# Norm statistics on VectorE or ScalarE, and new ranks for the strands of a two-layer kernel

## The chip, the cores and the metric

The kernel runs on one core of one Trainium2 chip. The metric is the device time of one execution in microseconds, as the median of several runs. A profile of one execution comes with it.

## The reference

Two transformer layers run one after the other over 16 sequences of 256 tokens with 128 features, 4096 tokens in all, in float32. Each half of a layer is followed by a residual sum and a layer norm:

```python
x = _layernorm(x + _L0_attn_ref(x, ...))   # RMS norm, 16 heads of 64, softmax over 256 keys, output projection
x = _layernorm(x + _L0_ffn_ref(x, ...))    # router, top 2 of 8 experts (hidden 256), one shared expert, exact gelu
x = _layernorm(x + _L1_attn_ref(x, ...))   # 16 heads of 8; each token attends over its own 16 heads
x = _layernorm(x + _L1_ffn_ref(x, ...))    # router, top 2 of 8 experts (hidden 512), exact gelu

def _layernorm(x, axis=-1, eps=1e-05):
    m = jnp.mean(x, axis=axis, keepdims=True)
    v = jnp.var(x, axis=axis, keepdims=True)
    return (x - m) / jnp.sqrt(v + eps)
```

The norm has neither scale nor shift, and its mean and variance go over the 128 features of a token.

## The kernel before

The tokens are cut into eight groups of 512. A group lies in SBUF as a tile `xg[g]` of 128 partitions by 4 chunks by 128 features, so that one chunk is 128 tokens, one on each partition. Layer 0's attention (`attention0`) goes through the groups in order, in 128 units: a unit is two heads of one sequence, with its scores, softmax, transposes and weighted values. `project` makes the output projection and `summed` adds the residual and calls the norm. The last group is cut in two halves (`project2`, `summed2`).

While attention still runs, finished groups go on to the experts of layer 0 in five waves (`wave`): the router chooses two experts for each token (`route`), `send` scatters the tokens' rows by indirect DMA from POOL into lists that are sorted by expert, `lists` runs the experts' matmuls over the lists, and `gathered` fetches the two results of each token and adds them. `middle` then calls the norm, layer 1's attention (`attention1`, with `chunk1` for each chunk, mostly products and sums on VectorE and POOL) and the second norm, and layer 1's experts follow in three waves (`wave1`, `last`), with the third norm and the store of the output. The second half of the last group goes through all experts without lists (`sequence`, `dense`).

All these are strands: Python generators that issue instructions for one step and then yield the time and the engine of their next one. `everything` is the planner. It keeps a clock for each engine (`clk`), booked by `work(engine, us, ...)` with a cost written into the code, and always continues the strand whose next step could start first; a strand's key is a rank and a time offset. The offset is taken off a strand's start when strands are compared, and ranks decide ties:

```python
best = min(starts, key=lambda c: (max(c[0] - c[1].key[0], first), c[1].key[1:]))[1]
```

The constants `KEYS` hold (rank, offset) for each kind of strand, `PACE` the offset of layer 0's heads in each half group. The order that comes out is the program order of every engine's queue, fixed when the kernel is built. Where a step may run on either of two engines, the planner's clocks decide: `copied` compares VectorE and ScalarE with `COPY` added to VectorE's side, `chunk1` gives products to POOL or VectorE by `FAVOUR` and lets TensorE make sums when it is `SUMS` behind VectorE, and `SWITCH` and `SWITCH_BACK` delay steps that need another activation table.

`normed(y, o, tag, at)` is called 36 times, nine in each of four places, for 32 chunks in each (128 in all; a call has four chunks or two). It takes its statistics on VectorE at L391 and L393, then `powered` adds eps at L377 on VectorE and raises to the power -0.5 at L381 on POOL, and the result is applied on VectorE (L399) or, after two small POOL operations (L405, L406), on ScalarE (L409). The RMS norm of layer 0 (`normalised`) sums its squares on ScalarE at L474, with the accumulator output. Softmax takes its maxima at L537 on VectorE and exponentials at L543 on ScalarE. The attention of layer 1 has products at L1216 and L1292 and sums at L1220 and L1267. L270 and L272 are the two roads of `copied`, L905 the scatter, L934 the gather, L948 the sum after a gather. PSUM has two buffers for each of its three tags "s", "t" and "m".

Of the kernel before, what the change touches and what calls it, by code (L numbers as in the profile page):

```python
# [9 lines left out]
FP = mybir.dt.float32  # L10
AF = mybir.ActivationFunctionType
ALU = mybir.AluOpType
# [3 lines left out]
P = 128  # L16
D = 128
# [20 lines left out]
def two_layers(  # L38
# [23 lines left out]
    nc = tc.nc  # L62
# [7 lines left out]
    sm = ctx.enter_context(tc.tile_pool(name="sm", bufs=2))  # L70
# [67 lines left out]
    def cleared(layer, w):  # L138
# [10 lines left out]

    INF = float("inf")  # L150
    KEYS = {
        "copy qk": (-0.897, 0.036),
        "copy v": (-2, 0.466),
        "copy p": (0.219, 0.818),
        "copy o": (-2, 0.246),
        "softmax": (-0.178, 0.347),
        "softmax 2": (-1.887, 0.235),
        "summed": (-1.203, 0.424),
        "normalised": (-0.822, 0.486),
        "heads": (-0.667, 0.044),  # L160
        "w route": (0.515, 0.015),
        "w send": (0.14, 0.346),
        "w shared": (-0.361, 0.219),
        "w loads": (-0.176, 0.409),
        "w turns 0": (-1.078, 0.086),
        "w turns 1": (1.714, 0.284),
        "w firsts 0": (-1.18, 0.141),
        "w firsts 1": (-0.671, 0.597),
        "w gelu": (-0.639, 0.186),
        "w seconds 0": (-0.71, 0.566),  # L170
        "w seconds 1": (-0.947, -0.095),
        "w stored": (-0.148, -0.464),
        "w gathered 0": (0.897, 0.302),
        "w gathered 1": (1.266, -0.485),
        "w qkv": (2, 0.577),
        "w attention1": (0.922, 0.081),
        "w attention1 2": (0.862, 0.231),
        "w sums": (0.434, 0.099),
        "w normed": (-1.109, 0.178),
        "d loads": (0.367, 1.088),  # L180
        "d route": (-0.611, 0.589),
        "d firsts": (-0.264, -0.008),
        "d gelu": (0.669, 0.244),
        "d seconds": (0.433, -0.444),
        "d added": (0.222, 0.651),
        "d normed": (-0.464, 0.567),
    }
    PACE = [0.305, 1.929, -0.337, -0.416, 1.268, -0.017, 0.106, 1.867]
    PACE += [1.673, 1.567, 1.23, 2, 1.49, 1.385, 1.46, 2]
    now = [0]  # L190
    COPY = -0.089
    SUMS = 9.857
    FAVOUR = 0.474
    SWITCH, SWITCH_BACK = 0.249, 0.734
    window, unit = [0, 0.0, 1.0], [P]
    clk = {"PE": 0.0, "DVE": 0.0, "ACT": 0.0, "POOL": 0.0, "SP": 0.0}
    table = ["exp"]
# [10 lines left out]
    def paced(at, us, mode):  # L208

        if mode != unit[0]:  # L210
            unit[0] = mode
            us += 0.09
        w = int(at / W)
        if w > window[0]:
            window[2] = 2.0 if w > window[0] + 1 or window[1] < 0.6 * W else 1.0
            window[:2] = w, 0.0
        us *= window[2]
        while at + us > (w + 1) * W:
            part = (w + 1) * W - at
            window[1] += part  # L220
            left = (us - part) / window[2]
            window[2] = 2.0 if window[1] < 0.6 * W else 1.0
            w, at, us = w + 1, (w + 1) * W, left * window[2]
            window[:2] = w, 0.0
        window[1] += us
        return at + us

    def work(e, us, *after, ports=False, one=None, mode=P):

        at = max(clk[e], floor[0], *after)  # L230
        if ports and pool[0] - 0.15 > at:
            us += min(pool[0] - 0.15 - at, pool[1])
        clk[e] = (paced(at, us, mode) if e == "PE" else at + us) + SETUP[e]
        if one is not None:
            pool[:] = clk[e], one
        return clk[e] + 0.08
# [23 lines left out]
    EITHER = ("DVE", "ACT")  # L260

    def copied(o, i, *after):
# [5 lines left out]
        dve, act = (max(clk[e], *after) + t for e, t in zip(EITHER, us))  # L268
        if dve + COPY <= act:
            nc.vector.tensor_copy(o, i)  # L270
# [102 lines left out]
    def powered(var, scale, eps, tag, at):  # L373

        n = var.shape[1]
        v = sm.tile([P, n], FP, tag=f"{tag}_v", name=f"{tag}_v", bufs=1 if tag == "ln0" else 2)
        nc.vector.tensor_scalar(v, var, scale, eps, ALU.mult, ALU.add)  # L377
        at = work("DVE", 0.2, at)
        yield at, "POOL"
        r = sm.tile([P, n], FP, tag=f"{tag}_r", name=f"{tag}_r", bufs=1 if tag == "ln0" else 2)  # L380
        nc.gpsimd.tensor_tensor(r, v, mhalf[:, 0:n], ALU.pow)  # L381
        return r, work("POOL", 1.1, at)

    def normed(y, o, tag, at):

        n = y.shape[1]
        yield at, "DVE"
        st = sm.tile([P, n, 6], FP, tag=f"{tag}_st", name=f"{tag}_st", bufs=1 if tag == "ln0" else 2)
        mv = sm.tile([P, n, 2], FP, tag=f"{tag}_mv", name=f"{tag}_mv", bufs=1 if tag == "ln0" else 2)
        for c in range(n):  # L390
            nc.vector.bn_stats(st[:, c, :], y[:, c, :])  # L391
        for c in range(n):
            nc.vector.bn_aggr(mv[:, c, :], st[:, c, :])  # L393
        at = work("DVE", 0.43 * n, at)
        r, at = yield from powered(mv[:, :, 1], 1.0, 1e-5, tag, at)
        yield at, EITHER
        if max(clk["DVE"], at) + 1.9 <= max(clk["ACT"], at) + 1.4:
            for c in range(n):
                nc.vector.tensor_scalar(  # L399
                    o[:, c, :], y[:, c, :], mv[:, c, 0:1], r[:, c : c + 1], ALU.subtract, ALU.mult  # L400
                )
            return work("DVE", 0.05 + 0.35 * n, at, ports=True)

        nb = sm.tile([P, n], FP, tag=f"{tag}_nb", name=f"{tag}_nb", bufs=1 if tag == "ln0" else 2)
        nc.gpsimd.tensor_tensor(nb, mv[:, :, 0], r, ALU.mult)  # L405
        nc.gpsimd.tensor_scalar(nb, nb, -1.0, 1.0, ALU.mult, ALU.mult)  # L406
        at = work("POOL", 0.4, at)
        for c in range(n):
            nc.scalar.activation(o[:, c, :], y[:, c, :], AF.Identity, bias=nb[:, c : c + 1], scale=r[:, c : c + 1])  # L409
        return work("ACT", 0.35 * n, at)  # L410
# [56 lines left out]
    def normalised(g):  # L467
# [10 lines left out]
        yield at, EITHER  # L478
        if max(clk["DVE"], at) + 1.2 + COPY <= max(clk["ACT"], at) + 1.4:
            for c in range(NC):  # L480
# [16 lines left out]
        hT[g] = sb.tile([P, GT], FP, tag="hT", name=f"hT{g}")  # L497
        if max(clk["DVE"], at) + 0.75 + COPY <= max(clk["ACT"], at) + 0.7:
            nc.vector.tensor_scalar(hT[g], t, nscale_s, None, ALU.mult)
# [136 lines left out]
    def summed(g, half, place, py, at):  # L636
        yield at, "DVE"
        nc.vector.tensor_tensor(ya[g], py, ya[g] if half else xg[g], ALU.add)
        at = closed(place, work("DVE", 0.75, at))
        if half:  # L640
            end["x", g] = yield from normed(ya[g], xg[g], "ln0", at)
# [16 lines left out]
    def summed2(b, place, py, at):  # L658
        yield at, "DVE"
        x = xg[LAST][:, 2 * b : 2 * b + 2, :]  # L660
        y = sb.tile([P, 2, D], FP, tag="ya", name=f"ya{LAST}_{b}", bufs=1)
        nc.vector.tensor_tensor(y, py, x, ALU.add)
        at = closed(place, work("DVE", 0.45, at))
        end["x", LAST, b] = yield from normed(y, x, "ln0", at)

    def attention0():
# [3 lines left out]
        for u in range(len(UNITS) + LAG):  # L670
# [4 lines left out]
            if g < NG:  # L675
                now[0] = 2 * g + i // NP
                running[-1].key = (KEYS["heads"][1], PACE[now[0]], 0, 0)
                if i == 3 and g + 1 < NG:
# [522 lines left out]
    def chunk1(w, c, o, qv, kv, at, sums):  # L1201
# [5 lines left out]
        for j in range(2):  # L1207
            yield (lambda: max(at, prod_ring.free(), sc_ring.free() if j == 0 else 0.0)), "DVE"
            if j == 0:
                sc1, ks = sc_ring.tile([P, NH1, NH1], "sc")  # L1210
                if "over" in end and clk["PE"] + SUMS < max(clk["DVE"], at) and ends["s"][-2] < clk["PE"] + 1.0:
                    ps = ps_s.tile([P, NH1, NH1], FP, tag="s", name="s1")
# [29 lines left out]
        if place is None:  # L1242
            yield at, ("POOL", "DVE")
            e, us = ("POOL", 0.6) if max(clk["POOL"], at) <= max(clk["DVE"], at) + FAVOUR else ("DVE", 0.4)
            (nc.gpsimd if e == "POOL" else nc.vector).tensor_tensor(
# [39 lines left out]
        for j in range(2):  # L1285
            yield (lambda: max(at, prod_ring.free())), ("POOL", "DVE")
            e, us = "POOL", 2.35
            if max(clk["DVE"], at) + 1.25 + FAVOUR < max(clk["POOL"], at) + 2.35:
                e, us = "DVE", 1.25
# [8 lines left out]
            at2 = work("POOL", us, at, one=us) if e == "POOL" else work("DVE", us, at, ports=True)  # L1298
            if j == 0 and "over" in end and clk["PE"] + SUMS < max(clk["DVE"], at) and ends["s"][-2] < clk["PE"] + 1.0:
                po = ps_s.tile([P, P], FP, tag="s", name="o1_sums")  # L1300
# [177 lines left out]
    w = DENSE  # L1478
# [185 lines left out]
```

## Time and profile before

| | before |
|---|---|
| median of 4 runs | 1225.72 us (1223.81 to 1227.38) |
| profiled execution | 1224.7 us |
| its span, first to last instruction | 1223.0 us |
| mean granted TensorE clock | 0.962 |
| busy: TensorE, VectorE, ScalarE, POOL | 1095.6, 911.1, 730.7, 701.8 us |
| norm statistics L391 | 64 + 32 + 32 instructions, 276 ns median |
| norm aggregates L393 | 96 + 32 instructions, about 150 ns median |
| activation table loads | 64, 1283 ns each |

The page of a profile gives busy time of each engine and its share of the span, then the span in 40 equal slices, where each digit is a busy share in tenths. Lines of a group name the kernel's line, the engine, the operation, its output and inputs and the count; behind the bar stand busy time, mean duration and the idle time before the group with what ended it. Matmul records are pipelined, so a busy TensorE need not be at its peak. Durations of neighbouring instructions of one engine can overlap, so a sequence is measured from its first start to its last end.

### The profile page before, as it was taken

How to read it: one execution, taken by the hardware profiler on the slowest of the kernel's cores; microseconds unless marked ns; L12 is line 12 of the kernel's file. 1: busy time of each engine (PE TensorE's matmuls, PEld its weight loads, DVE VectorE, ACT ScalarE, POOL GpSimd, SP SyncE). 2: the span in 40 equal slices, each digit the busy share in tenths (PEclk: the TensorE clock that was granted, in tenths of full speed). 3: DMA queues.
4: the chain of work that ended last, by engine and by line, in shares of the span. 5: the costliest groups of instructions: out<-in, count | busy, mean ns of one | idle time of the engine just before them, and what ended most of it. 6: DMA issues, size and time to landing. Idle time of an engine off the chain costs nothing.

```text
span 1223.0 us, 22539 instructions
## 1 busy us (share of the span) xinstructions
PE 1095.6 (90%) x7272; PEld 793.7 (65%) x7272; DVE 911.1 (75%) x1810; ACT 730.7 (60%) x2073; POOL 701.8 (57%) x1085
## 2 busy tenths in 40 slices
PE   9999999989999999988999998898667889778893
PEld 5566667666656665576655666675466879678792
DVE  4767786449889888864788888978886979896333
ACT  6556566667657756666566666765554655454441
POOL 4434363635565547732864775577684745476765
PEclk9999999999999999999999999999787989899997
DMA  8900021441000003043000033315627977975871
GB/s 266 274 1 1 1 83 57 143 117 56 6 1 1 2 1 93 29 127 92 30 1 2 16 106 104 94 46 168 189 87 235 282 213 216 273 218 170 248 227 58
DMA packets 187207, 132.45 MB, mean 108 GB/s; under 512 B 12745, under 2 KB 171474, under 8 KB 187090
## 3 DMA queue, kind: packets, MB, share of 16 engines
q1 hardware_dynamic: 179410, 115.27, 31.9%
q0 software_dynamic: 7680, 15.74, 4.1%
q8 instruction: 58, 0.95, 0.3%
q14 instruction: 59, 0.48, 0.1%
HBM read 97.94 MB, written 33.03 MB: 107 GB/s over the span
## 4 chain that ended last, share of the span: by engine, by line
PE 61%; DVE 13%; POOL 11%; ACT 7%; issue 4%; DMA 3%; SPq 1%; ACTq 0%; POOLq 0%; DVEq 0%
PE s L574 10%; PE po L612 9%; PE t L591 8%; POOL rows L905 7%; PE po_e L1118 4%; PE ph L1098 4%; PE pv L528 4%; PE pq L510 4%; PE py L629 3%; PE pk L510 3%; POOL pr L558 2%; DVE qk_prod L1216 2%; DVE av_prod L1292 2%; PE po_d L1541 1%; ACT h L1077 1%
## 5 line engine op out<-in xcount | busy, mean ns | idle before, releaser
L558 POOL TENSOR_SCALAR pr<-pr,rs 128x256 f32<-128x256 f32 x512 | 247.2, 502 | 258.2 <-DVE rs L554 169.6
L543 ACT ACTIVATE pr<-s,nm 128x256 f32<-128x256 f32 x512 | 236.1, 476 | 12.2 <-DVE nm L537 10.5
L537 DVE TENSOR_REDUCE nm<-s 128x4 f32<-128x1024 f32 x128 | 156.2, 1220 | 59.5 <-PE s L574 59.0
L1098 PE MATMUL ph<-xqT,wa 128*128 128x128 f32 x1028 | 142.5, 295 | 22.7 <-ACT h L1077 9.0
L905 POOL DMA_INDIRECT rows<-x,r_pi x120 | 132.1, 1101 | 39.5 <-issue 20.8
L1098 PEld LDWEIGHTS ph<-xqT,wa 128*128 128x128 f32 x1028 | 133.3, 206 | 32.2 <-ACT h L1077 11.6
L934 POOL DMA_INDIRECT y<-outs,r_pi x120 | 122.1, 1017 | 52.5 <-issue 22.6
L591 PE MATMUL t<-ident,pr 128*128 128x128 f32 x1024 | 141.8, 279 | 5.2 <-ACT pT L272 1.9
L591 PEld LDWEIGHTS t<-ident,pr 128*128 128x128 f32 x1024 | 111.4, 141 | 48.6 <-POOL pr L558 23.0
L612 PE MATMUL po<-pT,v 128*64 128x256 f32 x1024 | 140.5, 393 | 2.2 <-DVE kT L270 0.9
L270 DVE COPY pT<-t 128x512 f32<-128x512 f32 x171 | 111.6, 685 | 34.5 <-PE t L591 34.1
L574 PEld LDWEIGHTS s<-kT,qT 64*128 64x128 f32 x896 | 77.1, 186 | 82.3 <-issue 65.8
L574 PE MATMUL s<-kT,qT 64*128 64x256 f32 x896 | 127.1, 402 | 0.0
L272 ACT COPY oT<-po 128x256 f32<-128x256 f32 x102 | 38.0, 373 | 135.7 <-PE po L612 135.5
L543 ACT ACTIVATION_READ_ACCUMULATOR pr<-s,nm 128x1 f32 x512 | 106.0, 207 | 0.0
L1292 POOL TENSOR_TENSOR av_prod<-sc,qkv 128x1024 f32<-128x1024 f32 x34 | 86.2, 2545 | 29.3 <-ACT sc L1254 28.9
L612 PEld LDWEIGHTS po<-pT,v 128*64 128x64 f32 x1024 | 62.9, 136 | 61.8 <-issue 17.6
L1216 DVE TENSOR_TENSOR qk_prod<-qkv 128x1024 f32<-128x1024 f32 x64 | 83.0, 1297 | 0.0
L1267 DVE TENSOR_REDUCE o<-av_prod 128x64 f32<-128x1024 f32 x64 | 75.8, 1200 | 8.5 <-POOL av_prod L1292 8.2
L1118 PE MATMUL po_e<-wb,h 128*128 128x128 f32 x648 | 78.0, 279 | 2.0 <-DVE lg L738 1.5
L1220 DVE TENSOR_REDUCE sc<-qk_prod 128x128 f32<-128x1024 f32 x64 | 78.1, 1220 | 2.2
L1118 PEld LDWEIGHTS po_e<-wb,h 128*128 128x128 f32 x648 | 76.0, 195 | 3.6 <-DVE lg L738 1.9
(230 smaller groups left out, 1968.2 us busy)
## 6 DMA issues: line engine op xcount, KB each, us to landing
wa<-in_w_dram SPq DMA_DIRECT2D x190, 128.0 KB, 2.2
wa<-in_w_dram SPq DMA_DIRECT2D x81, 256.0 KB, 3.3
wb<-in_w_dram SPq DMA_DIRECT2D x81, 256.0 KB, 4.1
xq<-rows SPq DMA_DIRECT2D x38, 256.0 KB, 3.4
outs<-yq SPq DMA_DIRECT2D x38, 256.0 KB, 3.6
rows<-clear SPq DMA_DIRECT2D x3, 1472.0 KB, 11.6
rows<-clear SPq DMA_DIRECT2D x1, 2496.0 KB
rows<-clear SPq DMA_DIRECT2D x2, 1216.0 KB
```

The lines of the kernel that those rows point to most:

```text
L270: nc.vector.tensor_copy(o, i)
L537: nc.vector.tensor_reduce(nm[u], s, AX.X, ALU.max, negate=True)
L543: nc.scalar.activation(pr[u][:, i, :], s[:, i, :], AF.Exp, bias=nm[u][:, i : i + 1], accum_out=su[u][:, i : i + 1],)
L558: nc.gpsimd.tensor_scalar(pr[u][:, i, :], pr[u][:, i, :], rs[:, i : i + 1], 1.0, ALU.mult, ALU.mult)
L574: nc.tensor.matmul(sc[u][:, j, qc, :], q[part, ts(qc, P)], k[part, :], start=True, stop=True,)
L591: nc.tensor.transpose(t[:, kc, ts(qc, P)], pr[u][:, 2 * j + qc, ts(kc, P)], ident)
L612: nc.tensor.matmul(po[j * DH : (j + 1) * DH, :], vs[g, p // 4, 2 * b + kc][:, ts(h, DH)], pT[u][j][:, kc, :], start=(kc == 0), stop=(kc == 1),
L905: i = nc.gpsimd.indirect_dma_start(out=rows[layer][w][:, :], out_offset=bass.IndirectOffsetOnAxis(ap=r.pos[:, k, c : c + 1], axis=0), in_= ...
L934: nc.gpsimd.indirect_dma_start(out=y, out_offset=None, in_=outs[layer][w][:, :], in_offset=bass.IndirectOffsetOnAxis(ap=r.pos[:, k, c0 + c ...
L1098: nc.tensor.matmul(ph[:, q - q0, c, :], was[i, q][0][:, c, :], xTs[i][0][:, q, :], start=True, stop=True)
L1118: nc.tensor.matmul(po[:, q, :], hs[i, q][0][:, c, :], wbs[i, q][0][:, c, :], start=(c == 0), stop=(c == nh - 1))
L1292: (nc.gpsimd if e == "POOL" else nc.vector).tensor_tensor(m, sc1[:, ts(j, HALF)].unsqueeze(2).to_broadcast(full), v3.unsqueeze(1).to_broad ...
```

## The change

`normed` gets a second road for its statistics. If by the planner's clocks ScalarE would be through sooner, it makes two passes over each chunk there: Identity with a scale of -1/128 and the accumulator output, which gives the negative mean, and then Square with that as the bias and the accumulator output, which gives the sum of squares around the mean. `powered` then works on these sums, and the result is applied on VectorE or, after one POOL operation instead of two, on ScalarE. The constants of the planner are new.

```diff
     KEYS = {
-        "softmax": (-0.178, 0.347),
-        "softmax 2": (-1.887, 0.235),
-        "summed": (-1.203, 0.424),
+        "softmax": (0.123, 0.534),
+        "softmax 2": (-2, 0.288),
+        "summed": (-1.973, 0.291),
...
-        "w attention1": (0.922, 0.081),
-        "w attention1 2": (0.862, 0.231),
-        "w sums": (0.434, 0.099),
-        "w normed": (-1.109, 0.178),
+        "w attention1": (0.503, 0.205),
+        "w attention1 2": (0.398, 0.088),
+        "w sums": (-0.064, 0.324),
+        "w normed": (-0.698, 0.178),
...
     }
-    PACE = [0.305, 1.929, -0.337, -0.416, 1.268, -0.017, 0.106, 1.867]
-    PACE += [1.673, 1.567, 1.23, 2, 1.49, 1.385, 1.46, 2]
+    PACE = [1.119, 1.936, -0.517, -0.529, 1.723, 1.03, 0.706, 1.646]
+    PACE += [1.833, 1.427, 0.658, 0.868, 1.747, 1.411, 1.4, 0.455]
     now = [0]
-    COPY = -0.089
-    SUMS = 9.857
-    FAVOUR = 0.474
-    SWITCH, SWITCH_BACK = 0.249, 0.734
+    COPY = 0.465
+    SUMS = 8.497
+    FAVOUR = -0.257
+    SWITCH, SWITCH_BACK = 0.937, 0.586
...
     def normed(y, o, tag, at):
 
         n = y.shape[1]
-        yield at, "DVE"
+        yield at, EITHER
+        if max(clk["ACT"], at) + 1.0 * n < max(clk["DVE"], at) + 0.43 * n:
+
+            mm = sm.tile([P, 2, n], FP, tag=f"{tag}_mm", name=f"{tag}_mm", bufs=1 if tag == "ln0" else 2)
+            junk = sm.tile([P, D], FP, tag="junk", name="junk", bufs=1)
+            for c in range(n):
+                nc.scalar.activation(junk, y[:, c, :], AF.Identity, scale=-1.0 / D, accum_out=mm[:, 0, c : c + 1])
+            for c in range(n):
+                nc.scalar.activation(
+                    junk, y[:, c, :], AF.Square, bias=mm[:, 0, c : c + 1], accum_out=mm[:, 1, c : c + 1]
+                )
+            at = work("ACT", 1.0 * n, at)
+            yield at, "DVE"
+            r, at = yield from powered(mm[:, 1, :], 1.0 / D, 1e-5, tag, at)
+            yield at, EITHER
+            if max(clk["DVE"], at) + 1.9 <= max(clk["ACT"], at) + 1.4:
+                for c in range(n):
+                    nc.vector.tensor_scalar(o[:, c, :], y[:, c, :], mm[:, 0, c : c + 1], r[:, c : c + 1], ALU.add, ALU.mult)
+                return work("DVE", 0.05 + 0.35 * n, at, ports=True)
+            nb = sm.tile([P, n], FP, tag=f"{tag}_nb", name=f"{tag}_nb", bufs=1 if tag == "ln0" else 2)
+            nc.gpsimd.tensor_tensor(nb, mm[:, 0, :], r, ALU.mult)
+            at = work("POOL", 0.2, at)
+            for c in range(n):
+                nc.scalar.activation(o[:, c, :], y[:, c, :], AF.Identity, bias=nb[:, c : c + 1], scale=r[:, c : c + 1])
+            return work("ACT", 0.35 * n, at)
```

The ranks and offsets that are not shown change too, with few exceptions ("w normed" keeps its offset, as do "w route" and "w shared").

More of the change, by code (lines that the diff above doesn't have):

```diff
@@ L151, in two_layers @@
     KEYS = {
[L152 to L155, printed above, removed]
-        "softmax": (-0.178, 0.347),
-        "softmax 2": (-1.887, 0.235),
-        "summed": (-1.203, 0.424),
[L159 to L175, printed above, removed]
-        "w attention1": (0.922, 0.081),
-        "w attention1 2": (0.862, 0.231),
-        "w sums": (0.434, 0.099),
@@ L179, in two_layers @@
-        "w normed": (-1.109, 0.178),
[L180 to L186, printed above, removed]
-    }
-    PACE = [0.305, 1.929, -0.337, -0.416, 1.268, -0.017, 0.106, 1.867]
-    PACE += [1.673, 1.567, 1.23, 2, 1.49, 1.385, 1.46, 2]
+        "copy qk": (-0.847, 0.056),
+        "copy v": (-0.949, 0.45),
@@ new lines, in two_layers @@
+        "copy p": (-0.909, 1.173),
+        "copy o": (-2, 0.236),
+        "softmax": (0.123, 0.534),
+        "softmax 2": (-2, 0.288),
+        "summed": (-1.973, 0.291),
+        "normalised": (-0.552, 0.465),
+        "heads": (0.151, 0.076),
+        "w route": (-0.562, 0.015),
+        "w send": (0.933, 0.12),
+        "w shared": (-0.699, 0.219),
+        "w loads": (-1.173, -0.052),
+        "w turns 0": (-1.534, 0.391),
+        "w turns 1": (1.404, -0.009),
+        "w firsts 0": (-1.258, 0.123),
@@ new lines, in two_layers @@
+        "w firsts 1": (0.923, 0.481),
+        "w gelu": (-1.057, 0.15),
+        "w seconds 0": (-0.812, 0.175),
+        "w seconds 1": (0.374, 0.008),
+        "w stored": (-0.743, -0.471),
+        "w gathered 0": (1.066, 0.221),
+        "w gathered 1": (0.456, -0.214),
+        "w qkv": (1.457, 0.598),
+        "w attention1": (0.503, 0.205),
+        "w attention1 2": (0.398, 0.088),
+        "w sums": (-0.064, 0.324),
+        "w normed": (-0.698, 0.178),
+        "d loads": (-0.926, 1.021),
@@ L190, in two_layers @@
+        "d route": (0.806, 0.543),
+        "d firsts": (0.617, 0.244),
+        "d gelu": (0.187, 0.462),
+        "d seconds": (-0.474, -0.224),
+        "d added": (0.722, 0.759),
+        "d normed": (0.977, 0.804),
+    }
+    PACE = [1.119, 1.936, -0.517, -0.529, 1.723, 1.03, 0.706, 1.646]
+    PACE += [1.833, 1.427, 0.658, 0.868, 1.747, 1.411, 1.4, 0.455]
     now = [0]
-    COPY = -0.089
-    SUMS = 9.857
-    FAVOUR = 0.474
-    SWITCH, SWITCH_BACK = 0.249, 0.734
+    COPY = 0.465
+    SUMS = 8.497
```

## The prediction

> **What bounds the kernel now.** I read the page first, then busy time by stretches, then the timeline around the norms, then the chain of waits.
>
> ```profile
> span 1223.0 us, 22539 instructions
> PE 1095.6 (90%) x7272; PEld 793.7 (65%) x7272; DVE 911.1 (75%) x1810; ACT 730.7 (60%) x2073; POOL 701.8 (57%) x1085
> ...
> PE   9999999989999999988999998898667889778893
> ...
> DVE  4767786449889888864788888978886979896333
> ACT  6556566667657756666566666765554655454441
> ```
>
> The page's slices (30.6 us each) show two regimes. TensorE is at 9 nearly everywhere until slice 27; from there VectorE stands as high or higher. ScalarE never passes 7: it has room everywhere. The table by stretches gives the sizes (length, then busy PE, PEld, DVE, ACT, POOL, then the granted clock):
>
> ```profile
> 0.00:100.00 100.00, 97.13 (x574) 57.01 (x575) 62.79 (x103) 58.82 (x215) 42.37 (x107) 1.00 0.57 165
> 300.00:400.00 100.00, 97.24 (x613) 58.66 (x611) 86.62 (x146) 65.98 (x226) 60.12 (x95) 1.00 0.01 4
> 500.00:600.00 100.00, 90.38 (x601) 65.05 (x598) 66.00 (x113) 63.55 (x166) 48.23 (x64) 0.98 0.27 80
> 845.00:900.00 55.00, 36.13 (x190) 27.89 (x190) 46.33 (x121) 24.36 (x54) 37.38 (x60) 0.78 0.48 143
> 950.00:1000.00 50.00, 44.16 (x344) 40.66 (x343) 40.88 (x79) 29.91 (x50) 30.73 (x29) 0.97 0.84 253
> 1050.00:1100.00 50.00, 38.38 (x274) 33.93 (x272) 46.79 (x72) 26.03 (x45) 26.98 (x25) 0.90 0.87 255
> 1150.00:1223.00 73.00, 50.53 (x415) 49.05 (x414) 26.25 (x108) 25.97 (x52) 43.84 (x57) 0.87 0.52 154
> ```
>
> Until 845 us TensorE bounds: over all stretches of that table it is busy 803.5 of 845 us, idle 41.5. From 845 us it is busy 292.1 of 378 us, idle 85.9. From 845 to 1100 VectorE is busy 218.7 of 255 us (86%), ScalarE 133.4 (52%): there VectorE work is worth time. After 1100 neither is full and the chain runs through experts, gathers and the last norms.
>
> **Part 1, statistics that move to ScalarE.** The timeline around the first norm shows what is replaced (start, length):
>
> ```profile
> 103.43 0.69 DVE L638 TENSOR_TENSOR ya<-py,ya 128x512 f32<-128x512 f32 x1 [1.22 <-PE py L629]
> ...
> 104.15 0.88 DVE L391 BATCH_NORM_STATS2 ln_st<-ya 128x6 f32<-128x128 f32 x4
> ...
> 104.94 0.36 DVE L393 BATCH_NORM_AGGREGATE ln_mv<-ln_st 128x2 f32<-128x6 f32 x4
> ```
>
> Four statistics and four aggregates hold VectorE from 104.15 to 105.30, so 1.15 us for four chunks (the planner says 0.43 a chunk, 1.72). No row shows the two new passes; the nearest are the accumulating ScalarE passes in the chain that ended last:
>
> ```profile
> 3.60 1.29 ACT xn L474 x8
> 277.90 1.84 ACT pr L543 x8
> ```
>
> The first is four 128-wide squares with their accumulator reads and no bias operand, 1.29 us; the second four 256-wide exponentials with a bias per partition, 1.84 us. The new first pass is like L474: 1.3 us. The second has half the width of L543 and its bias: between 1.29 and 1.84, I take 1.5. A norm of four is thus 2.8 us on ScalarE (2.6 to 3.7) where the planner books 4.0, for 1.15 us freed on VectorE. Identity at L409 and Square at L474 cause no table load beyond the first of the program, so I cost none here. On the applying ScalarE road one POOL operation (L406, about 0.2 us) goes as well; the power on POOL stays. A wait is added: L377 on VectorE (0.24 us) now waits for ScalarE's second pass, and everything queued behind it on VectorE, in the attention of layer 1 the next product L1216, waits with it if ScalarE is late. Where ScalarE starts when planned, the wait is over before L377 comes up; each microsecond that it is late there is one that VectorE loses.
>
> A row against a rule: by these rows the move costs 2.8 us for 1.15 us, a loss unless VectorE is behind. The Trainium skill, "ScalarE: Activation LUTs", section "Rules for kernel authors", tells authors to give additions and multiplications to VectorE rather than ScalarE. By that rule this term would be zero or a loss.
>
> How often does it fire? The condition needs max(VectorE, y) to be over 0.57n us past max(ScalarE, y): 2.28 us for n=4, 1.14 for n=2. But VectorE itself writes y. In the timeline 30 of the 36 norms have their first L391 directly behind the instruction that wrote y, as here: 104.15 after 103.43+0.69. Of the other six only two lag by more than 0.91 us: 1.90 us at 1050.82 (n=2) and 3.21 us at 1120.13 (n=4). With the order of before the road would be taken about 0 to 2 times. The new ranks open it: the time offset of "w normed" stays 0.178 while "w attention1" goes from 0.081 to 0.205 and "w sums" from 0.099 to 0.324, so another chunk's product and sum (1.25 and 1.22 us, 2.47 together, over 2.28) may now stand before the statistics. That touches the 18 norms of layer 0's experts and layer 1's attention. The nine of "summed" need two softmax maxima (1.22 us each) ahead; the nine last ones run where VectorE is a third busy. I take 6 of 36 (0 to 18): 6 x 1.15 = 7 us off VectorE, 6 x 2.8 = 17 us onto ScalarE. About half of them lie in 845 to 1100, where VectorE counts; three norms and the wait they leave (the step after them starts sooner than behind a queue) make -3 us. The ends: 18 fired and all nine norms of that stretch (28 chunks, 0.29 us each) fully on the path, -8 us; none fired, 0; the losing end is the rival below.
>
> **Part 2, thresholds.** COPY from -0.089 to 0.465 asks VectorE to be 0.55 us sooner before it gets a copy. The groups put some 210 us of copies (L270) on VectorE, but nearly all before 845 us, where the copy only has to beat the next matmul; on the path I count -1 us (0 to -3). FAVOUR from 0.474 to -0.257 goes the other way: it takes products of attention from POOL to VectorE 0.73 us earlier. From 845 to 1100 VectorE already makes 17 av_prod at 1658 ns; POOL's take 2545 ns (L1292). Four more on VectorE are +6.6 us there and -10.2 us on POOL, where the scatters L905 form 17.2% of the chain from 845 us on. I take -1 us (-4 to +4). SUMS at 8.497 lets TensorE sum for VectorE at a smaller lead; before, all 64 reduces of each kind (L1220, L1267) were on VectorE, so it never fired at 9.857: 0, with -3 to +3 as ends. SWITCH from 0.249 to 0.937 delays a change to the gelu table; the page's groups hold 64 table loads of 1283 ns, 82 us of ScalarE, which has the room: 0.
>
> **Part 3, the order.** Nearly every rank moves, and PACE is lower in its last step (2 to 0.455) and higher in the first half. The bounds come from TensorE's idle time. The mixed stretches 200-300, 500-600 and 700-800 us idle 8.0, 9.6 and 9.7 us, the five other hundreds 2.5 on average. An order that made the three like the others would gain 20 us; one that made two or three more such stretches loses as much. The tail's 85.9 us can go either way by a tenth or two. No row tells the sign, so this term is 0, with -20 and +20 as ends.
>
> **Sum.** -3 -1 -1 +0 = -5 us against the profiled execution's 1224.7 us (span 1223.0 and 1.7 around it). The median, 1225.7, is 1.0 above it; on the median that makes 1220.7, which I round to 1220.5.
>
> **The rivals.**
> Slower: the new passes block ScalarE in the stretch that TensorE bounds. A norm of four holds ScalarE 2.8 us; behind it queue the copies that free the two-deep "m" and "t" PSUM buffers and the exponentials that free "s". A tile of L510 or L612 is 1.0 to 1.1 us of matmuls in the timeline, so TensorE runs out after some 1.5 us (one tile and what is left of the other) and stalls about 1.3 us. For it: TensorE idles only 2.5 us in a good hundred, so nothing hides a stall. Against it: ScalarE is 59 to 70% busy there, and copies may go to VectorE. Of 17 norms before 845 us eight stalling give +10 us: 1235.7; it outweighs the 5 us gain from four stalled norms on. A worse order adds its own part, up to 1245.
>
> No change: the road is hardly taken, since y's writer is VectorE itself, and the reordering cancels out: 1225.7, give or take 2.4.
>
> A stronger gain: a full -8 us from the norms and one mixed stretch as quiet as the others (-7): about 1210. It needs the nine norms in the tail all to move, so it is the thin end of the forecast's case.
>
> **How the numbers follow.** Forecast's case (tail relieved, including its strong end) 0.45; slower 0.43; no change 0.12. A measurement of this kernel tells about 0.2%, 2.4 us, from no change. The slower case stands nearly as high because the largest term, the order, has no sign in this profile and its ends are four times my sum. Within its own case the forecast spans 1210 to 1223. For 8 in 10 the range takes the order's gain to 1206 and the slower case to 1243.
>
> **What would show it.** In the profile after: two accumulating passes of Identity and Square, near 2.8 us for four chunks, and L391 fewer than 128 times, near 104; no further table loads; L1292 with more on VectorE and fewer on POOL; copies moved from L270 to L272; VectorE less than 218.7 us busy between 845 us and 1100. I am wrong in part 1 if L391 still counts over 120 or under 60; wrong in part 3 if the time before TensorE's share falls (845 us here) moves by more than the total does; and wrong in all if TensorE's idle time grows beyond 127 us.

## The result, and the profile after

Over 44 runs the kernel after the change takes 1225.33 us in the median, the kernel before 1226.88 us over 70 runs. The ratio is 0.9987 with a 95% interval of 0.9977 to 0.9997: 1.6 us saved (0.13% of 1226.9), where I had forecast 5. A second comparison (experiment 4) gave 0.9979 (0.9956 to 1.0001). The page of the profiled execution after (1228.27 us) shows, against the lines of before:

```profile
span 1225.6 us, 22553 instructions
PE 1105.6 (90%) x7272; PEld 795.4 (65%) x7272; DVE 850.1 (69%) x1716; ACT 782.2 (64%) x2178; POOL 678.9 (55%) x1054
...
PE   9999999999999999999998889898767888789895
...
DVE  3555534798845788763359886878998989968344
ACT  6667677667666676776876667666454755456533
```

VectorE lost 61 us of work, ScalarE gained 51, POOL lost 23. The total hardly moved. That alone does not tell whether VectorE's 61 us were worth nothing or whether ScalarE's 51 us ate their gain; experiments 1 and 3 ask for each by itself. The table by stretches (length, busy PE, PEld, DVE, ACT, POOL, then clock) shows where VectorE fell:

```profile
0.00:100.00 100.00, 97.67 (x571) 57.06 (x571) 49.78 (x78) 69.09 (x237) 41.70 (x104) 1.00 0.57 165
500.00:600.00 100.00, 98.90 (x669) 68.64 (x669) 48.96 (x92) 69.75 (x211) 34.66 (x63) 1.00 0.18 52
845.00:900.00 55.00, 38.39 (x197) 26.76 (x196) 46.84 (x128) 21.98 (x52) 39.38 (x62) 0.84 0.54 166
950.00:1000.00 50.00, 42.62 (x349) 39.96 (x350) 45.73 (x77) 31.94 (x51) 25.26 (x21) 1.00 0.87 263
1050.00:1100.00 50.00, 40.40 (x287) 36.24 (x286) 37.08 (x72) 23.24 (x39) 22.91 (x24) 0.93 0.72 216
1150.00:1223.00 73.00, 60.41 (x479) 57.99 (x477) 35.80 (x156) 28.67 (x54) 52.01 (x62) 0.94 0.62 185
```

It fell in the attention stretch, where TensorE bounds. From 845 to 1100 us VectorE is busy 221.2 us (46.84, 44.90, 45.73, 46.60, 37.08), 2.5 more than before (218.5 in a second profile of after, 0.2 less); the forecast's relief there did not come.

The reason for the first part of that is in the view of the statistics' own line (minimum, median and maximum in ns, first and last start):

```profile
L415 DVE BATCH_NORM_STATS2 n_st<-x x64: 269/276/291, 222.4 to 1216.6; 128x6 f32<-128x128 f32 x64
L415 DVE BATCH_NORM_STATS2 ln_st<-ya x32: 275/277/295, 104.6 to 861.8; 128x6 f32<-128x128 f32 x32
L415 DVE BATCH_NORM_STATS2 n_st<-y x32: 269/276/296, 352.0 to 1131.8; 128x6 f32<-128x128 f32 x32
```

All 128 statistics are still on VectorE, as before. The new road is taken in none of the 36 norms; cut out of the kernel after, with the yield for either engine kept, it leaves every queue's instructions and their order as they are. What moved is what the constants moved. The groups of the copies (count, then busy time, mean ns of one, and idle time before them) show it for the largest, first before, then after:

```profile
L270 DVE COPY pT<-t 128x512 f32<-128x512 f32 x171 | 111.6, 685 | 34.5 <-PE t L591 34.1
L272 ACT COPY pT<-t 128x512 f32<-128x512 f32 x85 | 47.7, 588 | 31.6 <-PE t L591 31.3
```

```profile
L272 ACT COPY pT<-t 128x512 f32<-128x512 f32 x162 | 89.9, 589 | 29.5 <-PE t L615 28.7 <-ACT pT L272 0.2
L270 DVE COPY pT<-t 128x512 f32<-128x512 f32 x94 | 61.7, 685 | 20.7 <-PE t L615 20.6
```

Of these 256 copies 77 went from VectorE to ScalarE. With the durations of all copies at L270 and L272 added up, VectorE's went from 221.3 to 124.7 us and ScalarE's from 214.5 to 298.5. In the waits VectorE's idle time before the softmax maxima, ended by TensorE's scores, went from 59.0 to 97.7 us: much of the freed time became waiting.

The last matmul of layer 0's output projection ends at 850.7 us before and at 861.1 after (855.2 in a second profile of after). From there to the end are 372.3 us before and 364.5 after (368.1). The new order loses 4.5 to 10.4 us in attention and wins 4.2 to 7.8 us in the tail, the part after it.

### The profile page after: what moved, and what is told of

It is laid out like the page before. It is cut to its first block, busy times and chain, and to the rows that moved or that the text cites. A ratio compares the mean times of both kernels' runs of the same rounds, so it can differ in the third digit from the quotient of the medians.

```text
span 1225.6 us, 22553 instructions
## 1 busy us (share of the span) xinstructions
PE 1105.6 (90%) x7272; PEld 795.4 (65%) x7272; DVE 850.1 (69%) x1716; ACT 782.2 (64%) x2178; POOL 678.9 (55%) x1054
## 4 chain that ended last, share of the span: by engine, by line
PE 53%; DVE 19%; POOL 13%; ACT 7%; issue 4%; DMA 3%; ACTq 0%; SPq 0%; POOLq 0%; DVEq 0%
PE s L598 8%; PE po L636 8%; PE t L615 7%; POOL rows L929 6%; PE py L653 4%; PE pv L552 4%; PE po_e L1142 3%; PE pq L534 3%; PE pk L534 3%; PE ph L1122 3%; DMA y<-outs,r_pi 3%; DVE av_prod L1316 3%; DVE o L1291 2%; DVE qk_prod L1240 2%; ACT pr L567 2%
## 5 line engine op out<-in xcount | busy, mean ns | idle before, releaser
L582 POOL TENSOR_SCALAR pr<-pr,rs 128x256 f32<-128x256 f32 x512 | 255.0, 515 | 278.7 <-DVE rs L578 229.4
L561 DVE TENSOR_REDUCE nm<-s 128x4 f32<-128x1024 f32 x128 | 155.9, 1218 | 98.4 <-PE s L598 97.7
L1122 PEld LDWEIGHTS ph<-xqT,wa 128*128 128x128 f32 x1028 | 130.6, 202 | 42.3 <-ACT h L1095 13.9
L929 POOL DMA_INDIRECT rows<-x,r_pi x120 | 128.7, 1072 | 50.2 <-DVE r_pi L877 27.8
L615 PE MATMUL t<-ident,pr 128*128 128x128 f32 x1024 | 145.5, 282 | 8.5 <-POOL pr L582 2.9
L636 PE MATMUL po<-pT,v 128*64 128x256 f32 x1024 | 144.6, 395 | 9.2 <-DVE v L270 3.9
L272 ACT COPY oT<-po 128x256 f32<-128x256 f32 x114 | 42.5, 373 | 109.6 <-PE po L636 109.2
L272 ACT COPY pT<-t 128x512 f32<-128x512 f32 x162 | 89.9, 589 | 29.5 <-PE t L615 28.7
L1316 POOL TENSOR_TENSOR av_prod<-sc,qkv 128x1024 f32<-128x1024 f32 x29 | 73.1, 2525 | 56.1 <-ACT sc L1278 55.9
L1240 DVE TENSOR_TENSOR qk_prod<-qkv 128x1024 f32<-128x1024 f32 x64 | 86.8, 1356 | 3.4 <-ACT qkv L272 3.4
```

What stands on the lines that cost most here:

```text
L272: nc.scalar.copy(o, i)
L561: nc.vector.tensor_reduce(nm[u], s, AX.X, ALU.max, negate=True)
L582: nc.gpsimd.tensor_scalar(pr[u][:, i, :], pr[u][:, i, :], rs[:, i : i + 1], 1.0, ALU.mult, ALU.mult)
L615: nc.tensor.transpose(t[:, kc, ts(qc, P)], pr[u][:, 2 * j + qc, ts(kc, P)], ident)
L636: nc.tensor.matmul(po[j * DH : (j + 1) * DH, :], vs[g, p // 4, 2 * b + kc][:, ts(h, DH)], pT[u][j][:, kc, :], start=(kc == 0), stop=(kc == 1),
L929: i = nc.gpsimd.indirect_dma_start(out=rows[layer][w][:, :], out_offset=bass.IndirectOffsetOnAxis(ap=r.pos[:, k, c : c + 1], axis=0), in_= ...
```

## The experiments

Ratios are to the kernel before in runs on the same chip, with 95% intervals. On two of the chips the kernel before itself took 1277 to 1280 us instead of 1226 to 1230, so microseconds are compared within a chip, and where the text compares across chips it says so.

**1. What the road costs and saves if it is taken.** The order of every queue is kept from the kernel after; only the engine of the statistics changes, with what hangs on it (the sign of the mean, and one POOL operation less), for the norms that a condition names (all, those issued after attention is over, those before). The lines are shortened, with comments of mine:

```diff
+        moved_over = "over" in end          # tail; True: all; "over" not in end: head
+        if moved_over:
+            # the two passes of the change on nc.scalar into mm
...
         at = work("DVE", 0.43 * n, at)      # still booked on VectorE, so the order stays
```

Tail:

> The kernel after the change, every queue in the same order, but the statistics of the 19 norms that are issued after layer 0's attention is over are made on ScalarE (two passes) instead of VectorE. Theory A (my prediction's part 1: VectorE's time is worth time from 845 to 1100 us): some 9 norms of that stretch free 8 us of VectorE and the total falls by 3 to 8 us. Theory B (the chain there runs through the norm itself, not through VectorE's load): each norm on the chain gets longer by 2.8 - 1.15 = 1.65 us, the total rises by 2 to 10 us. Both expect about 2.8 us from the first start to the last end of the two passes of four chunks.

Head:

> As tail_on_scalar, but for the 17 norms that are issued before layer 0's attention is over, while TensorE bounds. My rival (ScalarE's passes block the copies that free PSUM): +0.6 to 1.3 us for each, so +10 to +22 us. The other theory (buffers and copies on VectorE absorb it): within 3 us of the kernel after the change.

All:

> All 36 norms' statistics on ScalarE, order kept. If the two parts add up, the sum of the shifts of tail_on_scalar and head_on_scalar. Theory A: between -8 and +15 us; theory B: +5 to +30 us. VectorE loses 128 x 0.29 = 37 us of busy time in both, ScalarE gains 36 norms' passes, 90 us.

Measured: tail 1.0154 (1.0128 to 1.0180), head 1.0292 (1.0255 to 1.0329), all 1.0463 (1.0421 to 1.0504); the two parts add up to 4.5%, and together they cost 4.6%. So the road loses wherever it is forced, and by more than either theory allowed: some 20, 37 and 59 us, where the highest ends were 10, 22 and 30.

In the tail the wait that the prediction named is there. From the end of attention on, tail_on_scalar has this among VectorE's waits (us in total, times, longest), which the kernel after does not have:

```profile
DVE n_v L377 <- ACT junk L395: 59.3, 15, 7.7
```

How much of the tail's 20 us is this wait, and how much is ScalarE's other work that comes later behind the passes, no run separates.

For the head, ScalarE's part of the timeline around the first norm, with all norms moved:

```profile
105.54 0.30 ACT L393 ACTIVATE junk<-ya 128x128 f32<-128x128 f32 x1
...
105.96 0.31 ACT L393 ACTIVATE junk<-ya 128x128 f32<-128x128 f32 x1
...
107.27 0.40 ACT L395 ACTIVATE junk<-ya,ln_mm 128x128 f32<-128x128 f32 x1
...
109.15 0.19 ACT L395 ACTIVATION_READ_ACCUMULATOR junk<-ya,ln_mm 128x1 f32 x1
109.24 1.05 ACT L272 COPY pT<-t 128x512 f32<-128x512 f32 x2
```

The passes run from 105.54 to 109.34, 3.80 us, where I had put 2.8. Behind them come two copies of transposed probabilities, and TensorE's part of the same stretch shows who waited:

```profile
109.86 1.56 PE L627 MATMUL po<-pT,v 128*64 128x256 f32 x8 [1.52 <-ACT pT L272]
```

In the kernel after, the same matmuls start without a wait:

```profile
107.60 1.08 PE L636 MATMUL po<-pT,v 128*64 128x256 f32 x8
```

That is my rival's stall, 1.52 us against the 1.3 I had priced. With head_on_scalar attention ends at 894.9 us; in tail_on_scalar, on the same chip and with the order of after up to there, at 858.1. That is 37 us for 17 norms, 2.2 us each.

**2. Why the passes took 3.80 us.** All elementwise results of the passes, which nobody reads, go to one slice `junk`. Where the norm's result does not overwrite its input (12 of the 17 norms of the head), this kernel lets them go to the result's own four slices:

```diff
-            junk = sm.tile([P, D], FP, tag="junk", name="junk", bufs=1)
+            junk = [sm.tile([P, D], FP, tag="junk", name="junk", bufs=1)] * n if o is y else [o[:, c, :] for c in range(n)]
```

> head_on_scalar, but where a norm's result does not overwrite its input the two passes write their unused elementwise results to four separate slices (those of the result) instead of one shared slice, so that a pass need not wait for the write of the one before. If that wait is what made four chunks take 3.80 us, they come to 2.9 us or less (4 x 0.29 and 4 x 0.39 with the last read), and the loss against before falls from 2.9% to 2 to 2.5%. If the accumulator is what spaces them, 3.8 us stay and 1.029.

Measured 1.0190 (1.0165 to 1.0214), a little under the 2% that I had as the lower end; it ran on another chip than head_on_scalar. The same stretch of ScalarE's timeline:

```profile
105.06 0.30 ACT L393 ACTIVATE x<-ya 128x128 f32<-128x128 f32 x1
...
105.36 0.30 ACT L393 ACTIVATE x<-ya 128x128 f32<-128x128 f32 x1
...
107.38 0.39 ACT L395 ACTIVATE x<-ya,ln_mm 128x128 f32<-128x128 f32 x1
107.68 0.19 ACT L395 ACTIVATION_READ_ACCUMULATOR x<-ya,ln_mm 128x1 f32 x1
107.77 1.05 ACT L272 COPY pT<-t 128x512 f32<-128x512 f32 x2
```

The first passes now follow each other at 0.30 us instead of 0.43, and all eight take 2.81 us, which is the 2.8 that I had worked out from L474 and L543. Writing to one slice cost the other microsecond: nothing else in these instructions differs. Attention ends at 886.8 us; in small_step_b (below), on the same chip and with TensorE's order of after that far, at 858.7. The loss is still 28 us, 1.7 for each norm: 2.8 us of ScalarE for 1.15 of VectorE does not pay there even with own slices wherever the kernel has them.

**3. What VectorE's time is worth in the tail.** The statistics of the 19 tail norms are issued three times over:

```diff
+        for _ in range(3 if "over" in end else 1):
+            for c in range(n):
+                nc.vector.bn_stats(st[:, c, :], y[:, c, :])
+            for c in range(n):
+                nc.vector.bn_aggr(mv[:, c, :], st[:, c, :])
```

> The kernel after the change, order kept, with the VectorE statistics of the 19 norms after the attention issued three times over (the same result), so 2.3 us more of VectorE for each norm of four, some 37 us in all and 16 us of it between 860 and 1100 us. This is the slope that part 1 of my prediction took: if VectorE's time there is worth time one for one, +16 us or more; if half of it, +8; if VectorE's load is off the path and only the norms' own latency counts, +2.3 us for each norm on the chain, which I put at 3 to 5 norms: +7 to +12 us. The profile tells the last two apart by how far VectorE's idle time shrinks.

Measured 1.0003 (0.9973 to 1.0032). This kernel's runs scatter widely, from 1265 to 1290 us, and the median of all twelve is 1.0036 times that of before. From the end of attention VectorE is busy 309.0 us by the trace, where the kernel after has 277.6. The kernel after was not run on that chip; against its 0.998 to 0.999 of elsewhere this is some 2 to 7 us for 31 us of VectorE. So VectorE at 87 to 90% between 860 and 1100 us is busy, but it is not what the end waits for, microsecond for microsecond (+16 us). The lowest slopes, +7 and +8 us, are only just missed, and the two are not told apart. On the same chip and with the same order, moving the same 19 norms to ScalarE costs 1.5% more than tripling them on VectorE. Yet both make each norm of four longer by about as much, 2.3 us here and 2.65 there (3.80 less 1.15). So a longer norm does not by itself explain the tail's loss in experiment 1; that it is ScalarE which does the work matters.

**4. The constants one by one.** First the kernel after once more, on the chip of the three kernels that follow:

> The kernel after the change once more, on the same chip as the three kernels that follow, since chips differ. Expected: 0.997 to 1.000 of the kernel before.

Measured 0.9979 (0.9956 to 1.0001). Then the kernel before with the road and the yield for either engine alone, its constants untouched:

> The kernel before with only the new road and its changed yield in normed, all constants as before. In its list of instructions the road is taken 0 times (128 statistics on VectorE), but the yield for either engine moves later steps. Theory A (the change acts through the road): nothing can come of it, 1.000. Theory B (any reshuffle of the order moves the time by some tenths of a per cent, of either sign): 0.995 to 1.010, with no relation to the norms.

Measured 1.0439 (1.0409 to 1.0468), with all 128 statistics on VectorE. Then one constant, and then the ranks and paces without the thresholds:

```diff
-    COPY = -0.089
+    COPY = 0.465
```

> The kernel before with COPY = 0.465 alone: 362 copies on VectorE become 235, 401 on ScalarE become 522. My part 2 says -1 us (0 to -3), since TensorE bounds where nearly all of these copies are: 0.998 to 1.000. If VectorE's load had been what held TensorE up, some 90 us less of it would give 0.99 or less; if ScalarE comes to hold the exponentials up, over 1.003.

> The kernel before with the new KEYS and PACE alone, thresholds and norms as before. My part 3 put the order at 0 with -20 and +20 us as ends. If the small gain of the whole change is the order's, 0.996 to 0.999; if ranks and thresholds only work as a set that was tuned together, slower: 1.003 to 1.02.

Measured 1.0655 (1.0618 to 1.0692) and 1.0834 (1.0799 to 1.0870). With COPY alone the traces show 126 copies less at L270 and 126 more at L272 (415 to 541 on ScalarE, where my list had 401 to 522). On another chip, FAVOUR alone:

```diff
-    FAVOUR = 0.474
+    FAVOUR = -0.257
```

> The kernel before with FAVOUR = -0.257 alone; the waves keep their turns. My part 2 put it at -1 us with -4 and +4 as ends: 0.997 to 1.003. Narrow optimum: 1.01 to 1.05, like the other single edits.

Measured 1.0216 (1.0192 to 1.0240). Every part of the change that was tried alone costs 2 to 8%; the whole saves 0.1%. SUMS and the two SWITCH constants were not tried alone. None of my terms for the thresholds was above 4 us.

Last, the smallest steps around the kernel after, COPY at 0.45 and at 0.475 instead of 0.465:

> The kernel after with COPY = 0.45 in place of 0.465. The waves keep their turns; the program is the same up to row 834 of TensorE's 1738 listed rows and differs in places from there. Narrow optimum (the constants were found by trying and the best of many was kept): slower than the kernel before, 1.005 to 1.03. Flat: 0.996 to 1.001, as the kernel after.

> The kernel after with COPY = 0.475 in place of 0.465. The waves keep their turns and TensorE's order is the same up to row 1583 of 1738. Narrow optimum: 1.002 to 1.02; flat: 0.996 to 1.001.

Measured 1.0126 (1.0106 to 1.0145) and 1.0399 (1.0368 to 1.0430). The optimum is narrow: 0.01 in one constant of some ninety can cost 4%.

**5. What the lost per cents are.** In all three kernels of the first set of single edits the scatters of layer 1's first wave stand before those of layer 0's last wave in POOL's queue; in before and after they stand behind. One rule holds the order:

```diff
+        if w == len(WAVES[0]) - 1:
+            end["last routed"] = 0.0     # in wave, once it is routed
...
+        if w == 0:
+            yield after("last routed"), None     # in wave1, before its routing
```

Put into before or after the change, the rule alters no instruction. With it:

> before_with_copy with one rule more: layer 1's first wave may not be routed before layer 0's last wave is. In the kernels before and after the change that is the order anyway, and the rule alters no instruction of either; in before_with_copy, before_with_road and before_with_ranks layer 1's first wave was scattered first. Theory swap (nearly all of the 4 to 8% is this one change of turns): 0.99 to 1.01 of the kernel before. Theory tuned set (any reordering costs, since ranks fit only as a whole): 1.03 or more, as without the rule.

> before_with_road with the same rule. Theory swap: 0.99 to 1.01 instead of 1.044. Theory tuned set: 1.03 or more. It also gives the price of the changed yield alone, with the road never taken: my guess 1.00, plus or minus 0.007.

> before_with_ranks with the same rule. Theory swap: 0.99 to 1.015 instead of 1.083. Theory tuned set: 1.04 or more.

> The kernel after the change without the road and with the old yield of normed (VectorE alone), with the same rule, which it needs: without it its order scatters layer 1's first wave first. The constants of after are then tried on the norm of before. Theory swap: 0.99 to 1.01. Theory tuned set: 1.03 or more. If it is at or under the kernel after (0.998), the new yield was worth nothing.

Measured, in this order: 1.0227 (1.0205 to 1.0250), 1.0560 (1.0532 to 1.0587), 1.0588 (1.0555 to 1.0621) and 1.0542 (1.0514 to 1.0569). The turns explain 4.3 of COPY's 6.6 points and 2.5 of the ranks' 8.3, and with the road the rule made it worse. The theory holds in part only.

small_step_b has the right turns of routing and still loses 4%. There the other lock matters, the one on the expert lists. The gelu of layer 0's lists (L1101) in stretches shows when the last list ran, first in after, then in small_step_b (length, ScalarE busy on that line, clock, DMA):

```profile
900.00:930.00 30.00, 13.24 (x40) 0.84 0.28 89
930.00:960.00 30.00, 0.00 (x0) 0.94 0.84 257
```

```profile
900.00:930.00 30.00, 0.00 (x0) 0.71 0.29 91
930.00:960.00 30.00, 0.00 (x0) 0.52 0.21 65
960.00:990.00 30.00, 3.59 (x10) 0.69 0.62 182
990.00:1020.00 30.00, 9.57 (x31) 0.83 0.26 77
```

It starts 84 us later (984.6 against 900.9). Between 930 and 960 the DMA share is 0.21 against 0.84, and the granted clock falls to 0.52. SP's own waits in small_step_b from 855 to 1000 us say what held the loads up:

```profile
SPq L1021 <- DVE r_ei L891: 30.8, 1, 30.8
SPq L1038 <- DMA rows<-x,r_pi: 23.7, 1, 23.7
SPq L1497 <- PE po_d L1565: 21.0, 3, 20.0
```

In the kernel after the first of these is 6.4 us and the others are not among its longest. Layer 1's first wave has taken the lists' lock between two steps of layer 0's last wave; its list of experts (r_ei) and its 32 scatters are not ready. SP's loads go out in program order, so it waits for them with the other wave's loads behind: between 931 and 955 us it issues nothing. A rule that gives layer 0's last wave the lock first, again without effect on before or after:

```diff
+        if layer == 0 and w == len(WAVES[0]) - 1:
+            end["last listed"] = 0.0     # in lists, once the lock is held
...
+        if w == 0:
+            yield after("last listed"), None     # in wave1, before its lists
```

> small_step_b with one more rule: layer 1's first wave may not take the lock of the expert lists before layer 0's last wave has had it. In the kernels before and after the rule alters no instruction. Theory swap of the lists (the 90 us by which that list came late are what cost 4%): the list starts near 900 us and the ratio falls to 0.997 to 1.012. Theory narrow optimum without a single cause: 1.025 or more.

> after_old_yield_held (the constants of after on the norm of before, with VectorE alone) with the same rule on the lists. Theory swap of the lists: 1.00 to 1.02 instead of 1.054. Narrow optimum: 1.03 or more. If it comes to 0.998 or less, the version would beat both kernels without any road on ScalarE.

Measured 0.9948 (0.9921 to 0.9974) and 1.0261 (1.0218 to 1.0304). In lists_held the list runs where it belongs:

```profile
900.00:930.00 30.00, 11.71 (x34) 0.77 0.30 93
930.00:960.00 30.00, 1.78 (x7) 0.83 0.83 251
```

So small_step_b's 4% were this one inversion, shown by taking it away. The list's place is shown by the traces; the ratios come from two chips, each against before on its own, so the size of the gain is less sure. In after_old_yield_held it was 2.8 of 5.4 points, again across two chips; what the other 2.6 are stays open, as do the 5.6% of road_wave_held.

One regularity of these kernels was not followed up. In SP's program order, every kernel of experiments 4 and 5 that loses 2.6% or more loads the lists' rows in other turns than before and after do. Either layer 1's first wave has loads ahead of layer 0's last wave (before_with_road, before_with_copy, before_with_ranks, small_step_b, after_old_yield_held), or layer 1's last wave has loads ahead of the end of its second (before_with_ranks, road_wave_held, ranks_wave_held, old_yield_lists_held). The kernels at 1.023 or less (favour_alone, small_step_a, copy_wave_held, lists_held) keep the turns. So the first rule rid the road's kernel of the first kind and brought in the second. That the second kind is what the open per cents are fits, but no run took it away.

lists_held is 0.5% under before, but on one of the two chips where before takes about 1280 us, and after was not run there; whether it beats after is not settled.

## Why the prediction was wrong

**Part 1, the road.** "The new ranks open it ... I take 6 of 36 (0 to 18)" is the step that failed. The paragraph ahead of it had the right reading: VectorE writes y, so its clock is y's time, and the lead of 2.28 us is nearly never there. By the trace of after, 29 of the 36 norms have their first statistic within 0.04 us of the instruction that wrote y, and the other seven lag by 0.30 to 2.50 us; one lag is over 2.28 us (2.50 at 1067.96), and there too the road was not taken. The prediction's own sign of being wrong, L391 still over 120 times, came with 128. (Two of its lags were misread: at 1050.82 the statistics follow directly on L1559, which wrote y last, and at 1120.13 they lag 6.07 us behind L948. That leaves one lagging norm for two, and "about 0 to 2 times" stands.) From rank offsets I argued that other chunks would stand before the statistics; that needed a neighbour with work ready at that moment, which I had no row for. The term is 0, not -3 us, and in the sum this is most of the difference between -5 and -1.6. Its sign was wrong too: where the tail's 19 norms are moved by force, in experiment 1, they cost some 20 us. That the terms left, -2 us, come near the measured -1.6 is luck, since parts 2 and 3 do not hold term by term. The lower end, none fired, was in my text.

The price of the passes was right at 2.8 us for separate slices and 1.0 us too low for the code as written. The rule of the Trainium skill, "ScalarE: Activation LUTs", section "Rules for kernel authors", that additions and multiplications belong on VectorE rather than ScalarE, points the same way as experiment 1: 1.5 to 4.6% lost.

**VectorE's worth.** I counted a microsecond of VectorE between 845 and 1100 us as worth up to a microsecond. Experiment 3 added some 31 us (309.0 against 277.6), and the total rose by some 2 to 7 us. An engine at 86% was not the bound. What did move the tail by per cents was the order of waves, scatters and loads (experiment 5).

**Part 2.** For the whole change it held in kind: 97 us of copies left VectorE and the total moved by 1.6 us, SUMS moved no reduce (64 of each kind still), and table loads went from 64 to 62. FAVOUR moved nothing in the tail (18 av_prod on VectorE and 14 on POOL after the end of attention, in both). As prices of single edits the terms were worthless: COPY was put at -1 us and measured +6.6%, FAVOUR at -1 and +2.2%. Each also reshuffles the order: for COPY, holding one turn took back 4.3 of the 6.6 points.

**Part 3.** The total of 0 with -20 and +20 us as ends held, since order and thresholds together came out at -1.6 us. The reason was no insight: attention got 4.5 to 10.4 us longer and the tail 4.2 to 7.8 us shorter, and the two cancel. By the prediction's own sign (the time before TensorE's share falls moves by more than the total) part 3 was wrong. What in the order makes these two shifts, and so where the 1.6 us come from, was not tried. For other orders the ends were too narrow: +15 to +102 us. One thing that the tail hangs on was in the profile of before and I did not look for it: which wave's scatters and lists stand first.

**The rivals.** "No change", for the reason that y's writer is VectorE, is what happened, but for the 1.6 us; I gave it 0.12. The slower rival's mechanism is real where the road is forced (2.2 us each in the head against my 1.3), but the road is not taken, so it had nothing to act on.

## What to carry to other kernels

A choice between engines that compares planner clocks is only taken if the clocks can differ at that point: where one of the two engines has just written the input, count in the trace how often it is behind, and cost the option at zero if it never is. Where an order has been tuned as a whole, its gain is in the set; an option that is added shifts the order even if it is never taken (4.4% here), and what new constants give back must not be put down to the option. Of an order, look first at which long chain holds a lock or an in-order DMA queue: one wave that takes its turn with its data not ready cost 4% here, while 61 us less of VectorE's work went with a gain of 1.6 us.

## What the runs showed of the hardware

Accumulating ACTIVATEs of 128 elements without a bias operand follow each other at 0.30 us when their elementwise results go to different slices, and at 0.43 us when all go to the same one, although nobody reads it. In both cases the accumulator's read, an instruction of 0.19 us, starts 0.20 to 0.22 us after its ACTIVATE; with own slices the next ACTIVATE starts 0.10 us after that read's start, with the shared slice only when the read is over. The Trainium skill, "ScalarE: Activation LUTs", section "What ACT_TABLE_LOAD costs", has back-to-back ACTIVATEs overlap by about 93 ns. With own slices the read and the instruction behind it overlap by about as much (0.10 us at 107.77 in the rows of experiment 2). With the shared slice the read and the next pass do not overlap, though the read and the copy behind the last pass, which writes elsewhere, do (0.10 us at 109.24).

Two chips took about 50 us more for the same kernel, 1277 to 1280 against 1226 to 1230 us, at a granted clock of 0.944 to 0.953 in before's runs on one of them against 0.954 to 0.964 on one of the others. The attention part ends at the same time on one of the two as on the others (858.1 and 859.4 us against 855.2 and 861.1, for kernels that share its order), so it is the tail that is longer. Why was not tried.
